# Layer 1 of a two-layer graph network: head 0's product in 4 of 32 row tiles made by the scalar engine from logits to which a DMA adds adj

## The chip, the cores and the metric

One core of one Trainium2 chip. The metric is device time in microseconds (us) of one launch; the median of three runs of the kernel before is 3041.72 us. Times inside the launch come from one profiled execution and count from the start of its span.

Engine names are those of the profile: PE is the matrix engine (PEld its weight loads), DVE the vector engine, ACT the scalar engine, POOL the GpSimd engine, SP the engine that issues most loads. Each engine takes its instructions in the order in which they stand, and waits in that order.

## The reference, cut to what matters

`x` is 4096 x 512, `adj` a 4096 x 4096 matrix of zeros and ones. Two layers follow each other. Layer 0 is an attention with one head (`L0`); the change does not touch it. Layer 1 is a graph attention with 8 heads of 64 columns:

```python
h = jnp.maximum(_layernorm(x, axis=-1), 0.0)
data1 = (h @ W.T + b).reshape(N, H, D)
src = jnp.einsum('nhd,xhd->nh', data1, src_proj)
trg = jnp.einsum('nhd,xhd->nh', data1, trg_proj)
e = src.T[:, :, None] + trg.T[:, None, :]
e = jnp.where(e >= 0, e, 0.01 * e)
e = e + connectivity[None, :, :]      # connectivity is adj here
scores = jax.nn.softmax(e, axis=-1)
out = jnp.einsum('hnm,hmd->hnd', scores, data1.transpose(1, 0, 2))
x = x + out
```

So for each head, each target row n and each source row m the kernel needs the weight exp(leaky(src_n + trg_m) + adj[n, m]), its sum over m, and its product with the 64 values of row m. The exponential splits: exp(adj) is common to the heads, and leaky's two branches become a maximum of two products of row and column factors.

## The kernel before, in words

**Tiling of layer 1.** The output is cut into 4 blocks of 1024 target rows (`WL`) and 2 sets of 4 heads (`HG`): 8 *groups*, number i. In each group a loop goes over 32 tiles of 128 source rows; the tile number is m. A *step* is one (i, m). Source rows lie on the 128 partitions, the 1024 target rows on the free axis, so every weight tile is 128 x 1024 in fp32.

**One step.** `load` (L668, SP) brings the tile of `adj_t` (512 KB) into one of three buffers `e`. `exps` (L682, ACT) makes ex = exp(adj) into PSUM; the pool `p_x` has one buffer, so ex of step m + 1 can't be written before DVE has read ex of step m for the last time. `last_exps` (L692, ACT) makes e3 = exp(adj + a column) for head 3 into SBUF. `relus` (L698, ACT) makes `rl`, a relu of head 0's row factors with a scale and a bias of one column each. `weigh` (DVE) makes the four products `pr0` to `pr3` in the order of heads 3, 0, 1, 2: L710 is (z max g) * ex, with e3 in place of ex for head 3, and L707 is (rl - ngd) * ex for head 0. Each is one instruction on 128 x 1024.

**Sums.** POOL adds up head 3's products over the steps (L719, accumulator `acc3`). Head 0's products are added up by accumulating DMAs from POOL's queue (L724, L726) into `acc00` and `acc01` in the 19 steps of `BY_DMA`: m from 2 to 26 without those with m % 4 == 1. In the other 13 steps PE takes the sum.

**gather** (PE) multiplies the four products with the values (L742, 16 matmuls that the trace records as 32 passes, banks `pv`), then takes the sums of heads 1 and 2, and of head 0 where no DMA does (L747, bank `dn`). The products of heads 3 and 0 come first, those of heads 1 and 2 after them.

**Buffers.** `pr0` and `pr3` have three buffers, `pr1` and `pr2` two; `rl`, `e3` and `acc3` two.

**Order.** It is written out by hand; nothing is planned by costs:

```python
stages = ((load, 3), (exps, 1), (weigh, 1), (factors, 2), (scale, 2), (gather, 0))
for s in range(len(steps)):
    for f, ahead in stages:
        if s + ahead < len(steps):
            f(*steps[s + ahead])
    ...
    next(ending, None)
```

`factors` is `last_exps` and then `relus`. So while DVE works at the products of step m, ACT's queue holds ex(m), e3(m+1), rl(m+1), in groups 0 and 1 two short `scale` instructions (L678), and then whatever `ending` yields. In group 0 `ending` is `tables`, which writes row factors to DRAM (`z_d`); later groups' factors are read from there by `zload` at m = 20, 22, 24, 26 (SP). In every later group it is `finish` of the group before: ACT copies `pv` (L771) and `dn` (L777) out of PSUM in the first two steps, PE makes two transposes a step, and ACT makes four short scaled copies `o` (L821) a step behind the products of steps 4 to 11; POOL issues four accumulating loads of `x1` into `o` (L824). `finish_last` ends the last group.

Of the kernel before, what the change touches and what calls it, by code (L numbers as in the profile page):

```python
# [8 lines left out]
FP = mybir.dt.float32  # L9
AF = mybir.ActivationFunctionType  # L10
ALU = mybir.AluOpType
# [4 lines left out]
P = 128  # L16
# [3 lines left out]
SLOPE = 0.01  # L20


def row_bcast(ap, n, offset=0):

    return bass.AP(tensor=ap.tensor, offset=ap.offset + offset, ap=[[0, P], [1, n]])
# [3 lines left out]
def kernel(  # L29
# [15 lines left out]
    nc = tc.nc  # L45
    N, F = x.shape
    H, D = 8, 64
    HG, WL = 4, 1024
    WT = WL // P
    NT = N // P  # L50
# [6 lines left out]
    dram = ctx.enter_context(tc.tile_pool(name="dram", bufs=1, space=DRAM))  # L57
    ident = const.tile([P, P], FP, name="ident")
# [3 lines left out]

    x1 = dram.tile([N, F], FP, name="x1")
    z_d = dram.tile([H * NT, P], FP, name="z_d")

# [11 lines left out]
    s_n = big.tile([P, H, NT], FP, name="s_n")  # L79
    t_m = big.tile([P, H, NT], FP, name="t_m")  # L80
# [15 lines left out]
    with tc.tile_pool(name="w0", bufs=1) as wp, tc.tile_pool(name="a0", bufs=2) as ap_, tc.tile_pool(  # L96
        name="a0s", bufs=8
# [144 lines left out]
    with tc.tile_pool(name="mx", bufs=1) as mxp, tc.tile_pool(name="b_a", bufs=6) as adjp, tc.tile_pool(  # L242
        name="b_e", bufs=4
    ) as esp, tc.tile_pool(name="b_m", bufs=2) as mkp, tc.tile_pool(name="b_s", bufs=2) as sp, tc.tile_pool(
        name="b_p", bufs=6, space=PSUM
# [56 lines left out]
        for n in range(-6, len(items)):  # L302
# [3 lines left out]
            if n >= 0:  # L306
                i, j, t = items[n]
# [9 lines left out]
    with tc.tile_pool(name="c_a", bufs=11) as adjp, tc.tile_pool(name="c_b", bufs=4) as ebp, tc.tile_pool(  # L317
        name="c_e", bufs=9
    ) as etp, tc.tile_pool(name="c_w", bufs=3) as wkp, tc.tile_pool(name="c_t", bufs=3) as atp, tc.tile_pool(
        name="c_m", bufs=2  # L320
    ) as mxp, tc.tile_pool(name="c_o", bufs=4) as iop, tc.tile_pool(name="c_s", bufs=2) as sp, tc.tile_pool(
        name="c_p", bufs=1, space=PSUM
    ) as p_o, tc.tile_pool(name="c_q", bufs=3, space=PSUM) as p_t, tc.tile_pool(
        name="c_r", bufs=1, space=PSUM
# [102 lines left out]
        left, scale = [], {}  # L427
# [81 lines left out]
        tmb = big.tile([P, H], FP, name="tmb")  # L509
# [38 lines left out]
        stages = ((load, 8), (turn, 3), (exps, 2), (weigh, 1), (gather, 0))  # L548
# [22 lines left out]
        pt = p_t.tile([P, BL], FP, name="pt")  # L571
# [15 lines left out]
    l1 = ctx.enter_context(tc.tile_pool(name="l1", bufs=1))  # L587
# [2 lines left out]
    d_m = l1.tile([P, H, NT], FP, name="d_m")  # L590
    ngd_m = l1.tile([P, H // HG, NT], FP, name="ngd_m")
    ld_m = l1.tile([P, H // HG, NT], FP, name="ld_m")
    d0_m = l1.tile([P, H // 2, NT, 2], FP, name="d0_m")
    d0_0 = l1.tile([P, H // 2, P // 4], FP, name="d0_0")
    zo = l1.tile([P, 3], FP, name="zo")
# [14 lines left out]

    HV = WL // BL
    JT = BL // P
    Q = P // 4
    BY_DMA = [m for m in range(2, NT - 5) if m % 4 != 1]

    with tc.tile_pool(name="p", bufs=2) as prp, tc.tile_pool(name="rl", bufs=2) as rlp, tc.tile_pool(
        name="io1", bufs=3
    ) as iop, tc.tile_pool(name="s1", bufs=1) as sp, tc.tile_pool(name="za", bufs=1) as zp0, tc.tile_pool(name="e3", bufs=2) as e3p, tc.tile_pool(  # L620
        name="zb", bufs=1
    ) as zp1, tc.tile_pool(name="e", bufs=3) as ep, tc.tile_pool(name="ac", bufs=2) as acp, tc.tile_pool(
        name="os", bufs=1
    ) as osp, tc.tile_pool(
        name="p_x", bufs=1, space=PSUM
    ) as p_x, tc.tile_pool(name="p_v", bufs=1, space=PSUM) as p_v, tc.tile_pool(
        name="p_t1", bufs=1, space=PSUM
    ) as p_t, tc.manual_schedule():
        groups = [(b, g) for b in range(N // WL) for g in range(H // HG)]
        steps = [(i, m) for i in range(len(groups)) for m in range(NT)]  # L630
        zs_, ra, ex, e3, rl, pr, acc, pv, late = {}, {}, {}, {}, {}, {}, {}, {}, {}
        ORDER = (3, 0, 1, 2)
        for t, val in ((d0_0, 0.0), (d0_m, 0.0), (zo[:, 0:2], 0.0), (zo[:, 2:3], 1.0)):
# [2 lines left out]
        def tables():  # L636

            for h in range(H):
                nc.scalar.activation(s_n[:, h, :], s_n[:, h, :], AF.Relu, bias=tmb[:, h:h + 1])
                if h % 3 == 2:  # L640
                    yield
            nc.scalar.activation(s_n, s_n, AF.Exp, scale=-(1.0 - SLOPE))
            yield
            s_f = s_n.rearrange("p h t -> p (h t)")
            for c in range(H * NT // P):
                pz = p_t.tile([P, P], FP, name="pt")
                nc.tensor.transpose(pz, s_f[:, c * P:(c + 1) * P], ident)
                yield
                zt = sp.tile([P, P], FP, name="zt", bufs=2)
                nc.scalar.copy(zt, pz)  # L650
                nc.gpsimd.dma_start(z_d[c * P:(c + 1) * P, :], zt)
            yield


        pick = sp.tile([P, 2, 4], FP, name="pick")
        row = ident.rearrange("p (r s) -> p s r", s=Q)
        nc.vector.tensor_copy(pick, row[:, 0:2, :])
        nc.vector.tensor_tensor(pick[:, 1, 0:HV], pick[:, 1, 0:HV], row[:, 2, HV:2 * HV], ALU.add)

# [5 lines left out]
        def load(i, m):  # L665
            b, g = groups[i]
            e = ep.tile([P, WL], FP, name="e")
            nc.sync.dma_start(e, adj_t[m * P:(m + 1) * P, b * WL:(b + 1) * WL])  # L668
            ra[i, m] = e
            if i + 1 < len(groups) and m in (20, 22, 24, 26):  # L670
                zload(i + 1, ORDER[(m - 20) // 2])

# [16 lines left out]
        def last_exps(i, m):  # L689
# [2 lines left out]
            nc.scalar.activation(x_, ra[i, m], AF.Exp, bias=ld_m[:, h // HG, m:m + 1])  # L692
            e3[i, m] = x_

        def relus(i, m):
            h = groups[i][1] * HG
            r = rlp.tile([P, WL], FP, name="rl")
            nc.scalar.activation(r, zs_[i, 0], AF.Relu, bias=ngd_m[:, h // HG, m:m + 1], scale=d_m[:, h, m:m + 1])  # L698
            rl[i, m] = r

        def weigh(i, m, order=ORDER):
            h = groups[i][1] * HG
            x_ = ex.pop((i, m))
            for k in order:
                w = prp.tile([P, WL], FP, name=f"pr{k}", bufs=2 if k in (1, 2) else 3)
                if k == 0:
                    nc.vector.scalar_tensor_tensor(w, rl.pop((i, m)), ngd_m[:, h // HG, m:m + 1], x_,  # L707
                                                   op0=ALU.subtract, op1=ALU.mult)
                else:
                    nc.vector.scalar_tensor_tensor(w, zs_[i, k], g_m[:, h + k, m:m + 1],  # L710
                                                   e3.pop((i, m)) if k == 3 else x_,
                                                   op0=ALU.max, op1=ALU.mult)
                pr[i, m, k] = w
            w = pr[i, m, 3]
            if m == 1:
                acc[i, 3] = acp.tile([P, WL], FP, name="acc3")
                nc.gpsimd.tensor_tensor(acc[i, 3], pr[i, 0, 3], w, ALU.add)
            elif 1 < m < NT - 1:
                nc.gpsimd.tensor_tensor(acc[i, 3], acc[i, 3], w, ALU.add)  # L719
            if m in BY_DMA:  # L720
                n = BY_DMA.index(m)
                if n < 2:
                    acc[i, 0, n] = acp.tile([P, WL], FP, name=f"acc0{n}", bufs=1)
                    nc.gpsimd.dma_start(acc[i, 0, n], pr[i, m, 0])  # L724
                else:
                    nc.gpsimd.dma_start(acc[i, 0, n % 2], pr[i, m, 0], accum_op=ALU.add)  # L726

        def gather(i, m):
            b, g = groups[i]
            last = m == NT - 1  # L730
            if m == 0:
                pv[i] = ([[p_v.tile([P, BL], FP, name=f"pv{c}{q}") for q in range(HV)] for c in range(2)],
                         p_v.tile([P, BL], FP, name="dn"))
            v, dn = pv[i]
            by_pe = [u for u in range(NT) if u not in BY_DMA]
            side = sum(u < m for u in by_pe) % 2
            for c, pair in enumerate(((3, 0), (1, 2))):
                for q in range(HV):
                    for r in (side, 1 - side):
                        k = pair[r]  # L740
                        for c0 in range(0, D, Q):
                            nc.tensor.matmul(v[c][q][r * D + c0:r * D + c0 + Q, :],  # L742
                                             va[:, m, g * HG + k, c0:c0 + Q],
                                             pr[i, m, k][:, q * BL:(q + 1) * BL], start=(m == 0), stop=last)

            def den(r, w, src, q, **fl):
                nc.tensor.matmul(dn[r * Q:r * Q + w.shape[1], :], w, src[:, q * BL:(q + 1) * BL], **fl)  # L747

            for r in (side, 1 - side):
                for q in range(HV):  # L750
                    hk = g * 2 + r
                    den(r * HV + q, d0_m[:, hk, m, :] if m else d0_0[:, hk, :], pr[i, m, r + 1], q,
                        start=(m == 0), stop=False)
            if m in by_pe:
                for q in range(HV):
                    den(side * HV + q, zo[:, 1 - side:3], pr[i, m, 0], q, start=False, stop=False)
# [126 lines left out]

        def row_factors(k):
            z = zs_[0, k]
            nc.vector.tensor_scalar(z, z, tmb[:, k:k + 1], 0.0, ALU.add, ALU.max)
            nc.scalar.activation(z, z, AF.Exp, scale=-(1.0 - SLOPE))

        row_factors(3)
        nc.vector.tensor_tensor(t_m, t_m, tmb.unsqueeze(2).to_broadcast([P, H, NT]), ALU.subtract)  # L890
        nc.vector.tensor_scalar(ld_m, t_m[:, HG - 1::HG, :], SLOPE, None, ALU.mult)
        nc.scalar.activation(g_m, t_m, AF.Exp, scale=1.0 - SLOPE)
        last_exps(0, 0)
        del ra[0, 0]
# [12 lines left out]
        factors(0, 1)  # L907
        scale(0, 1)

        stages = ((load, 3), (exps, 1), (weigh, 1), (factors, 2), (scale, 2), (gather, 0))  # L910
        for s in range(len(steps)):
            for f, ahead in stages:
                if s + ahead < len(steps):
# [44 lines left out]
```

## Time and profile before

| | us |
|---|---|
| median of three runs | 3041.72 (3041.07 to 3043.09) |
| the profiled execution's own time | 3042.05 |
| its span, first to last instruction | 3040.3 |
| first product of layer 1 | at 1791.7 |
| group 0 (m = 0 of one group to m = 0 of the next) | 154.7 |
| group 1 | 154.6 |
| groups 2 to 6, each | 153.7 |

The granted TensorE clock is 0.995 in the mean. The page gives busy times and shares of the whole span; layer 1 is its last 41%. In a row of a group, "x512 | 631.1, 1273" means 512 instructions, 631.1 us in which at least one of them ran, 1273 ns for one from start to end. Instructions of one engine overlap: the next starts before the last has ended, so the pace is read from start to start in the timeline, not from the duration.

### The profile page before, as it was taken

Reading aid. Unit: us, or ns where it says so; the run is one execution under the profiler, and the core shown is the slowest. Engines: PE = TensorE matmul, PEld = TensorE weight load, DVE = VectorE, ACT = ScalarE, POOL = GpSimd, SP = SyncE. Lnnn points to the kernel's source line nnn. Section 1 sums busy time; section 2 is a strip of 40 time slices with the busy share of each in tenths; the row PEclk is TensorE's granted clock in tenths of the full one; section 3 lists DMA queues with packets and bytes.
Section 4 is the critical chain, followed back from the end, with each engine's and each line's share of the span. In section 5 each row is a group of like instructions: output and inputs, shape, how many; then the busy total and the mean of one; then the engine's idle time right before and its main releaser. Section 6 shows DMA issues by size and latency. Waiting matters only on the chain.

```text
span 3040.3 us, 43210 instructions
## 1 busy us (share of the span) xinstructions
PE 2988.8 (98%) x15817; PEld 1204.4 (40%) x15817; DVE 2517.5 (83%) x3515; ACT 1292.0 (42%) x1819; POOL 1332.7 (44%) x1009
## 2 busy tenths in 40 slices
PE   8999999999999999999999989999999999999998
PEld 4444444444444444444444433323222222222222
DVE  5335777777677687887987789999999999999998
ACT  2111111111111121121122367887777777777775
POOL 3401111113333343443544656564656564656564
PEclk9999999999999999999999999999999999999999
DMA  4205666666444454554543238595959596968685
GB/s 152 97 4 195 223 220 224 233 211 216 139 161 161 148 175 134 173 168 142 185 167 119 63 112 213 170 230 173 233 172 232 176 227 177 228 178 224 181 216 139
DMA packets 226645, 531.51 MB, mean 175 GB/s; under 512 B 24888, under 2 KB 50520, under 8 KB 226432
## 3 DMA queue, kind: packets, MB, share of 16 engines
q1 hardware_dynamic: 178048, 384.12, 37.9%
q0 software_dynamic: 46368, 140.70, 19.6%
q10 hardware_dynamic: 2016, 3.93, 0.4%
q8 instruction: 124, 2.03, 0.3%
q14 instruction: 89, 0.73, 0.1%
HBM read 389.02 MB, written 59.93 MB: 148 GB/s over the span
## 4 chain that ended last, share of the span: by engine, by line
PE 69%; DVE 19%; ACT 6%; issue 4%; DMA 1%; DVEq 0%; SPq 0%; POOL 0%; ACTq 0%; POOLq 0%
PE po L419 29%; DVE pr L710 16%; PE pe L284 15%; PE pv L742 8%; ACT e L692 4%; PE ps L155 4%; PE po L489 4%; PE pe L162 4%; PE dn L747 3%; DVE pr L707 2%; PE pt L369 2%; ACT rl L698 1%; PE pt L797 1%; PE pt L143 0%; PE pt L481 0%
## 5 line engine op out<-in xcount | busy, mean ns | idle before, releaser
L742 PE MATMUL pv<-pr,sup 128*32 128x512 f32 x8192 | 1010.1, 595 | 17.2 <-DVE pr L710 8.4
L419 PE MATMUL po<-sup,at 128*128 128x512 f32 x2048 | 905.5, 594 | 2.8 <-DVE at L389 2.8
L719 POOL TENSOR_TENSOR acc<-acc,pr 128x1024 f32<-128x1024 f32 x232 | 555.9, 2396 | 391.3 <-DVE pr L710 390.1
L710 DVE SCALAR_TENSOR_TENSOR pr<-z,g_m,ex 128x1024 f32<-128x1024 f32 x512 | 631.1, 1273 | 3.7 <-PE dn L747 3.7
L419 PEld LDWEIGHTS po<-sup,at 128*128 128x128 f32 x2048 | 379.0, 191 | 428.6 <-issue 417.0
L399 POOL TENSOR_TENSOR racc<-racc,ex 128x512 f32<-128x512 f32 x240 | 343.0, 1429 | 452.2 <-ACT ex L383 451.0
L742 PEld LDWEIGHTS pv<-pr,sup 128*32 128x32 f32 x8192 | 287.1, 110 | 609.2 <-issue 494.9
L383 ACT ACTIVATE ex<-d 128x512 f32<-128x512 f32 x256 | 160.6, 630 | 722.8 <-DVE d L381 715.6
L682 ACT ACTIVATE ex<-e 128x1024 f32<-128x1024 f32 x256 | 263.5, 1029 | 305.4 <-DVE pr L710 305.4
L284 PE MATMUL pe<-he_t,he_t 128*128 128x512 f32 x896 | 386.4, 592 | 0.0
L707 DVE SCALAR_TENSOR_TENSOR pr<-rl,ngd_m,ex 128x1024 f32<-128x1024 f32 x256 | 326.0, 1273 | 3.3 <-ACT ex L682 3.0
L747 PE MATMUL dn<-pr,d_m 128*2 128x512 f32 x1984 | 327.3, 592 | 0.0
L710 DVE SCALAR_TENSOR_TENSOR pr<-z,g_m,e 128x1024 f32<-128x1024 f32 x256 | 326.4, 1275 | 0.2 <-ACT e L692 0.2
L698 ACT ACTIVATE rl<-z,ngd_m,d_m 128x1024 f32<-128x1024 f32 x256 | 314.3, 1228 | 0.0
L692 ACT ACTIVATE e<-e,ld_m 128x1024 f32<-128x1024 f32 x256 | 290.5, 1135 | 0.0
L381 DVE TENSOR_TENSOR d<-d,mk 128x512 f32<-128x512 f32 x256 | 269.3, 1052 | 8.8
L284 PEld LDWEIGHTS pe<-he_t,he_t 128*128 128x128 f32 x896 | 169.2, 190 | 210.1 <-issue 190.8
L287 ACT COPY es<-pe 128x512 f32<-128x512 f32 (+2 forms) x144 | 79.3, 551 | 377.0 <-PE pe L284 377.0
L288 POOL DMA_DIRECT2D e_d<-es x144 | 78.6, 546 | 364.6 <-ACT es L287 358.9
L380 DVE TENSOR_TENSOR d<-pt,mb 128x512 f32<-128x512 f32 (+2 forms) x136 | 87.4, 643 | 166.5 <-PE pt L369 166.5
L389 DVE TENSOR_TENSOR at<-ex,a 128x512 f32<-128x512 f32 x256 | 175.6, 686 | 23.1 <-ACT ex L383 21.3
L289 DVE CUSTOM_DVE_ANT_0 mk<-pe,mk 128x512 f32<-128x512 f32 (+2 forms) x144 | 93.0, 646 | 99.6 <-ACT es L287 99.6
(162 smaller groups left out, 2546.4 us busy)
## 6 DMA issues: line engine op xcount, KB each, us to landing
e<-in_adj_t_dram SPq DMA_DIRECT2D x256, 512.0 KB, 4.6
acc<-pr POOLq DMA_DIRECT2D x152, 512.0 KB, 5.2
a<-in_adj_t_dram SPq DMA_DIRECT2D x256, 256.0 KB, 3.1
ar<-in_adj_dram SPq DMA_DIRECT2D x120, 256.0 KB, 3.1
e_d<-es POOLq DMA_DIRECT2D x120, 256.0 KB, 3.2
ac<-in_adj_t_dram SPq DMA_DIRECT2D x112, 256.0 KB, 3.7
eb<-e_d SPq DMA_DIRECT2D x28, 1024.0 KB, 6.3
et<-e_d SPq DMA_DIRECT2D x112, 256.0 KB, 3.3
```

The source lines that it names most:

```text
L284: nc.tensor.matmul(pe[:, :w], he_t[i][:, k, (t % TB) * P:(t % TB + 1) * P], he_t[j][:, k, BL - w:], start=(k == 0), stop=(k == KC - 1))
L381: nc.vector.tensor_tensor(d, d, mk, ALU.add)
L399: nc.gpsimd.tensor_tensor(racc, racc, e, ALU.add)
L419: nc.tensor.matmul(po[j], w[:, j * P:(j + 1) * P], sup[:, m, :], start=(m == 0), stop=last)
L682: nc.scalar.activation(x_, ra.pop((i, m)), AF.Exp)
L692: nc.scalar.activation(x_, ra[i, m], AF.Exp, bias=ld_m[:, h // HG, m:m + 1])
L698: nc.scalar.activation(r, zs_[i, 0], AF.Relu, bias=ngd_m[:, h // HG, m:m + 1], scale=d_m[:, h, m:m + 1])
L707: nc.vector.scalar_tensor_tensor(w, rl.pop((i, m)), ngd_m[:, h // HG, m:m + 1], x_, op0=ALU.subtract, op1=ALU.mult)
L710: nc.vector.scalar_tensor_tensor(w, zs_[i, k], g_m[:, h + k, m:m + 1], e3.pop((i, m)) if k == 3 else x_, op0=ALU.max, op1=ALU.mult)
L719: nc.gpsimd.tensor_tensor(acc[i, 3], acc[i, 3], w, ALU.add)
L742: nc.tensor.matmul(v[c][q][r * D + c0:r * D + c0 + Q, :], va[:, m, g * HG + k, c0:c0 + Q], pr[i, m, k][:, q * BL:(q + 1) * BL], start=(m = ...
L747: nc.tensor.matmul(dn[r * Q:r * Q + w.shape[1], :], w, src[:, q * BL:(q + 1) * BL], **fl)
```

## The change

In steps m = 9, 13, 17, 21 of every group (`BY_LOG`) head 0's product is made in another way. `logs` makes, three steps ahead, the relu part of the logit from a row tile `u` and a column (`nlg_m`) on ACT, and an accumulating DMA from POOL's queue adds the tile of `adj_t` to it in SBUF. In `weigh`, ACT takes the exponential of that with a column as bias and writes it as `pr0`; DVE makes no product for head 0 in these steps, and `relus` is left out in them. The rest of these steps, ex and the load of `e` among it, stays.

The row tile `u` holds the relu before its exponential. For group 0 it is kept from `row_factors`; for the later groups `tables` writes it to DRAM (`u_d`: two transposes, one copy and one DMA more, and one `yield` more), and it is read back into one buffer at m = 28 of the group before, by SP.

Buffers: `pr3` goes from three to two, `acc3` from two to one, `rl` from two to three. PE's work is the same: the four steps are among those in which PE takes head 0's sum anyway.

```diff
+    u_d = dram.tile([2, NT, P], FP, name="u_d")
...
+    nlg_m = l1.tile([P, H // HG, NT], FP, name="nlg_m")
...
+    BY_LOG = (9, 13, 17, 21)
     BY_DMA = [m for m in range(2, NT - 5) if m % 4 != 1]
 
-    with tc.tile_pool(name="p", bufs=2) as prp, tc.tile_pool(name="rl", bufs=2) as rlp, tc.tile_pool(
+    with tc.tile_pool(name="p", bufs=2) as prp, tc.tile_pool(name="rl", bufs=3) as rlp, tc.tile_pool(
...
-    ) as osp, tc.tile_pool(
+    ) as osp, tc.tile_pool(name="u", bufs=1) as usp, tc.tile_pool(
...
+            pz = p_t.tile([P, 2, P], FP, name="pt")
+            for g in range(H // HG):
+                nc.tensor.transpose(pz[:NT, g, :], s_n[:, g * HG, :], ident)
+            yield
+            ut = sp.tile([NT, 2, P], FP, name="ut")
+            nc.scalar.copy(ut, pz[:NT])
+            nc.gpsimd.dma_start(u_d.rearrange("g t p -> t g p"), ut)
             nc.scalar.activation(s_n, s_n, AF.Exp, scale=-(1.0 - SLOPE))
...
+            if i + 1 < len(groups) and m == 28:
+                us[i + 1] = usp.tile([P, WL], FP, name="u")
+                b, g = groups[i + 1]
+                nc.sync.dma_start(us[i + 1], row_bcast(u_d, WL, g * N + b * WL))
...
+        def logs(i, m):
+            if m in BY_LOG:
+                b, g = groups[i]
+                r = rlp.tile([P, WL], FP, name="rl")
+                nc.scalar.activation(r, us[i], AF.Relu, bias=nlg_m[:, g, m:m + 1], scale=-(1.0 - SLOPE))
+                nc.gpsimd.dma_start(r, adj_t[m * P:(m + 1) * P, b * WL:(b + 1) * WL], accum_op=ALU.add)
+                rl[i, m] = r
+
         def relus(i, m):
+            if m in BY_LOG:
+                return
...
-                w = prp.tile([P, WL], FP, name=f"pr{k}", bufs=2 if k in (1, 2) else 3)
-                if k == 0:
+                w = prp.tile([P, WL], FP, name=f"pr{k}", bufs=3 if k == 0 else 2)
+                if k == 0 and m in BY_LOG:
+                    nc.scalar.activation(w, rl.pop((i, m)), AF.Exp, bias=t_m[:, h, m:m + 1])
+                elif k == 0:
                     nc.vector.scalar_tensor_tensor(w, rl.pop((i, m)), ngd_m[:, h // HG, m:m + 1], x_,
                                                    op0=ALU.subtract, op1=ALU.mult)
...
-                acc[i, 3] = acp.tile([P, WL], FP, name="acc3")
+                acc[i, 3] = acp.tile([P, WL], FP, name="acc3", bufs=1)
...
         def row_factors(k):
             z = zs_[0, k]
-            nc.vector.tensor_scalar(z, z, tmb[:, k:k + 1], 0.0, ALU.add, ALU.max)
-            nc.scalar.activation(z, z, AF.Exp, scale=-(1.0 - SLOPE))
+            u = z
+            if k == 0:
+                u = us[0] = usp.tile([P, WL], FP, name="u")
+            nc.vector.tensor_scalar(u, z, tmb[:, k:k + 1], 0.0, ALU.add, ALU.max)
+            nc.scalar.activation(z, u, AF.Exp, scale=-(1.0 - SLOPE))
...
+        nc.vector.tensor_scalar(nlg_m, t_m[:, 0::HG, :], -(1.0 - SLOPE), None, ALU.mult)
...
-        stages = ((load, 3), (exps, 1), (weigh, 1), (factors, 2), (scale, 2), (gather, 0))
+        stages = ((load, 3), (logs, 3), (exps, 1), (weigh, 1), (factors, 2), (scale, 2), (gather, 0))
```

In a step of `BY_LOG` ACT's queue then reads ex(m), the exponential for `pr0` (called *w* below), e3(m+1), rl(m+1); the relu of `logs` for step m (called *log*) stands ahead of ex(m-2), its DMA on POOL between the instructions for step m-3 and the addition for step m-2.

More of the change, by code (lines that the diff above doesn't have):

```diff
@@ L630 @@
         steps = [(i, m) for i in range(len(groups)) for m in range(NT)]
+        us = {}
         zs_, ra, ex, e3, rl, pr, acc, pv, late = {}, {}, {}, {}, {}, {}, {}, {}, {}
```

## The prediction

> **What bounds the kernel now.** I read the page first, then the stretches of single groups, then the timeline of one group engine by engine. The page:
>
> ```profile
> PE 2988.8 (98%) x15817; PEld 1204.4 (40%) x15817; DVE 2517.5 (83%) x3515; ACT 1292.0 (42%) x1819; POOL 1332.7 (44%) x1009
> ...
> L742 PE MATMUL pv<-pr,sup 128*32 128x512 f32 x8192 | 1010.1, 595 | 17.2 <-DVE pr L710 8.4
> L710 DVE SCALAR_TENSOR_TENSOR pr<-z,g_m,ex 128x1024 f32<-128x1024 f32 x512 | 631.1, 1273 | 3.7 <-PE dn L747 3.7
> L682 ACT ACTIVATE ex<-e 128x1024 f32<-128x1024 f32 x256 | 263.5, 1029 | 305.4 <-DVE pr L710 305.4
> L707 DVE SCALAR_TENSOR_TENSOR pr<-rl,ngd_m,ex 128x1024 f32<-128x1024 f32 x256 | 326.0, 1273 | 3.3 <-ACT ex L682 3.0
> ```
>
> DVE's products in layer 1 wait for almost nothing (3.7 and 3.3 us in all), PE nearly as little (17.2), while ACT idles 305 us, all before ex, released by DVE. So DVE is the bound with PE close behind, and ACT looks free. How free is seen in the timeline of one plain step (m = 17 of group 4), DVE and then ACT; columns are start, time, engine, line, operation:
>
> ```profile
> 2490.66 1.28 DVE L710 SCALAR_TENSOR_TENSOR pr<-z,g_m,e 128x1024 f32<-128x1024 f32 x1
> 2491.86 1.27 DVE L707 SCALAR_TENSOR_TENSOR pr<-rl,ngd_m,ex 128x1024 f32<-128x1024 f32 x1
> 2493.05 2.46 DVE L710 SCALAR_TENSOR_TENSOR pr<-z,g_m,ex 128x1024 f32<-128x1024 f32 x2
> 2495.43 1.27 DVE L710 SCALAR_TENSOR_TENSOR pr<-z,g_m,e 128x1024 f32<-128x1024 f32 x1
> ```
> ```profile
> 2490.77 1.03 ACT L682 ACTIVATE ex<-e 128x1024 f32<-128x1024 f32 x1 [1.54 <-DVE pr L710]
> 2491.73 1.13 ACT L692 ACTIVATE e<-e,ld_m 128x1024 f32<-128x1024 f32 x1
> 2492.77 1.23 ACT L698 ACTIVATE rl<-z,ngd_m,d_m 128x1024 f32<-128x1024 f32 x1
> 2495.54 1.03 ACT L682 ACTIVATE ex<-e 128x1024 f32<-128x1024 f32 x1 [1.54 <-DVE pr L710]
> ```
>
> A step lasts 4.77 us, four products of 1.19 from start to start. ACT's ex starts 0.11 after the step does, because the single buffer of ex is free only then, and the next ACT instructions follow at 0.96, 1.04 and (in the steps of `finish`, below) 1.13. DVE's head 0 product starts at 1.20, when ex ends at 1.14: ex is on the path with 0.05 us to spare, hidden by one product alone. ACT's real freedom is the 1.54 us between rl and the next ex. In the steps of `finish` it is less:
>
> ```profile
> 2458.80 1.23 ACT L698 ACTIVATE rl<-z,ngd_m,d_m 128x1024 f32<-128x1024 f32 x1
> 2459.93 0.90 ACT L821 ACTIVATE o<-pt,rd 128x64 f32<-128x64 f32 x4
> 2461.56 1.03 ACT L682 ACTIVATE ex<-e 128x1024 f32<-128x1024 f32 x1 [0.73 <-DVE pr L710]
> ```
>
> The four o take 0.80 at their pace of 0.20. PE's place: in group 4 the first pass of gather(m) starts 2.73 us after step m when PE has nothing to catch up (m = 22 to 25). The transposes of `finish` push that to 7.96 at m = 10; then it falls by 0.48 a plain step (4.29 us of PE work against 4.77) and is 3.00 at m = 21. Once in a group PE is so late that DVE waits for the buffer of pr1, at m = 12:
>
> ```profile
> 2469.18 2.47 DVE L710 SCALAR_TENSOR_TENSOR pr<-z,g_m,ex 128x1024 f32<-128x1024 f32 x2 [0.49 <-PE dn L747]
> ```
>
> From the step's length (5.35 for 4.77) that costs 0.57.
>
> **The change, part by part.** Times below count from the start of the step named.
>
> *Products removed.* 4 x 1.19 = 4.77 us of DVE a group, 38 us in eight groups. How much of it reaches the end is decided by ACT.
>
> *The exponential w in ACT's queue.* It stands between ex(m) and e3(m+1). Its nearest row is L692 (exponential, SBUF to SBUF, column bias): 1.04 from start to start; the ends are L682's 0.96 and L698's 1.13, worth 0.1 each way. The step on DVE now lasts 3 x 1.19 = 3.58, and the next ex should start at 3.69. ACT is done with its queue at 0.11 + 0.96 + 1.04 + 1.04 + 1.13 = 4.28. DVE waits 0.59 at its next head 0 product, and a plain log step saves 1.19 - 0.59 = 0.60. That holds for m = 13, 17, 21: 1.8 us a group.
>
> *m = 9 falls into `finish`.* w adds the four o: the queue ends at 5.08, a stall of 1.39, more than the 1.19 saved. The relu of log(9), 1.13 us by L698, stands before ex(7): 0.11 + 0.96 + 1.04 + 1.13 + 0.80 + 1.13 = 5.17 against 4.88, a stall of 0.28; that of log(13) before ex(11) costs 0.29 in the same way. The logs for 17 and 21 fit into the 1.54. Together 1.96 lost around m = 9.
>
> *The wait at m = 12 goes.* DVE gets there 1.96 - 1.19 = 0.77 later, PE no later than before (its 5 us of arrears at m = 9, 10 cover the delay), so the 0.57 is not waited.
>
> Sum for groups 2 to 7: 4.77 - 1.77 - 1.96 + 0.57 = 1.6 us each, 9.7 in six. PE permits about this and little more: with its 4.29 a plain step and 4.72 for one with head 0's sum, it catches up with the faster DVE at m = 26 instead of 21, and from 27 on needs 4.72 of 4.77 a step.
>
> *Groups 0 and 1* have the two `scale` instructions behind rl, 0.5 us. Group 0: each w stalls 1.09, so 4 x (1.19 - 1.09) = 0.4, less 0.1 for a log beside a table copy: 0.3 gained. Group 1 has scale and o both: stalls 0.77 (log 9), 1.89 (w at 9), 0.79 (log 13), 3 x 1.09, in all 6.7 against 4.77; its own waits for PE at m = 8 to 12, 1.06, go. It loses 0.9. The new column table at the start costs DVE some 0.15.
>
> *The accumulating load.* POOL issues it after the addition for step m-3, which ends at 3.8, and that step's own 0.86 us DMA:
>
> ```profile
> 2482.55 2.39 POOL L719 TENSOR_TENSOR acc<-acc,pr 128x1024 f32<-128x1024 f32 x1 [1.58 <-DVE pr L710]
> 2484.90 0.85 POOL L726 DMA_DIRECT2D acc<-pr  x1
> ```
>
> So at 4.7, when the relu is done too; POOL is free until 6.2, so the addition behind it isn't delayed. w wants the sum at 1.07 of step m, that is 10.7 us later. What rows exist for the landing:
>
> ```profile
> e<-in_adj_t_dram SPq DMA_DIRECT2D x256, 512.0 KB, 4.6
> acc<-pr POOLq DMA_DIRECT2D x152, 512.0 KB, 5.2
> o<-x POOLq DMA_DIRECT2D x28, 256.0 KB, 7.5
> ```
>
> Same size and accumulating: 5.2, the low end. The high end is o<-x, which accumulates from DRAM as this does, 7.5 for half the bytes, doubled to 15. I take 9.0, nearest to the acc row: 5.2, plus 2.2 for the acc transfer issued just ahead (q0: 140.70 MB in 19.6% of the span, 4.2 us a MB), plus 1.6 for an e load between (q1: 37.9% for 384 MB). That lands 1.7 us early and costs nothing. Four such loads add 8.9 us of DMA to 153.7, to a share of 0.76.
>
> *Parts at nothing.* u's load is SP's 28th-step extra; SP idles over 3 us a step and u is wanted ten steps later. `acc3` with one buffer: the first addition of a group starts at 2414.71, the last pass that reads the old sums ends at 2413.53. `pr3` with two buffers would wait where PE is latest, up to 0.7 at m = 10, and ACT's stall of 1.39 on the product after it covers that. Without ACT's stalls these 0.7 would be paid. The additional table work in group 0 lies where PE and ACT have room.
>
> A rule that speaks against the change: the Trainium skill, "SBUF — State Buffer", section "Who interferes with whom", says that a DVE instruction with two SBUF inputs and a GpSimd instruction that reads SBUF exclude each other. Head 3's product (z and e3 both in SBUF) never meets POOL's addition in this trace, since it starts at 4.77 and the addition ends at 3.8; in log steps it would start at 3.58. By the rule it waits 0.24, in 32 steps 7.7 us; but head 0's next product waits for ex until 5.37 anyway, so I get the same sum by rule and by row.
>
> **Sum.** 9.7 + 0.3 - 0.9 - 0.15 = 8.9 us. The profiled execution's 3042.05 gives 3033.1; it stands 0.33 above the median of the runs, so from the median 3032.8.
>
> **Rivals.** (1) *ACT's instructions are dearer.* w waits for several semaphores and might cost L698's whole 1.23: 0.19 more in 32 steps takes 6 us, and 3039 is left. For: no row shows such an instruction. Against: L692's pace. (2) *The accumulating load lands late*, and w blocks ACT, with e3, rl and the next ex queued behind it and DVE behind these. One us late is 32 us: 3065; at the doubled o<-x landing (15, 4.3 late) 3170. It decides from 8.9 / 32 = 0.28 us of mean lateness, a landing at 11.0. For: DMA share 0.78 in a group's first half, o<-x's 7.5. Against: the acc row, and that o<-x moves 1 KB pieces where this moves 4 KB ones. (3) *The whole DVE saving arrives*, 38 us, 3003.6. Against: ACT's queue, and PE, whose spare time after m = 21 is about 2 us a group.
>
> **How the numbers follow.** Some 0.2% (6 us) is what a measurement of this kernel can tell from no change. The forecast has 0.57, (1) 0.19, (2) 0.20, (3) 0.04. Faster by over 0.2%: the forecast and (3), 0.61; within 0.2%: (1) 0.19; slower: (2) 0.20. The range runs from 3028 (ACT at its cheap end, PE's limit of about 2 us a group) past (1), 3039, to 3046, which is (2) with 0.4 us of mean lateness; what is left out is the rest of (2) and (3).
>
> **What would show it right or wrong.** Right: log steps of 3.58 and next ones of 5.36; the idle time before L682 falls by some 40 us, DVE's waits for ex rise by about 33 (6 x 3.7, 4.5 and 6.7); groups 2 to 6 last 152.1, group 1 155.5; m = 10 lasts over 6 us if PE doesn't hold m = 9. Wrong: a wait of ACT's w for the DMA (rival 2), groups above 153.7; or DVE's waits for PE in place of those for ex, with groups near 152; or log steps followed by 4.77 (rival 3).

## The result, and the profile after

The changed kernel takes 3039.65 us (median of 12 runs, 3036.68 to 3044.28); the kernel before, timed beside it, 3041.55 (12 runs, 3041.07 to 3043.32). The ratio is 0.9992 with an interval of [0.9983, 1.0001]: a gain of 1.9 us, within what can't be told from no change, where 8.9 were forecast. The profiled execution took 3040.68 us, its span is 3038.8.

The page after, the groups that answer to those of before (L739 is the product pr = (z max g) * ex, L736 head 0's product, L699 ex, L709 e3):

```profile
PE 2988.1 (98%) x15819; PEld 1206.2 (40%) x15819; DVE 2487.0 (82%) x3484; ACT 1317.7 (43%) x1852; POOL 1362.1 (45%) x1042
...
L739 DVE SCALAR_TENSOR_TENSOR pr<-z,g_m,ex 128x1024 f32<-128x1024 f32 x512 | 631.3, 1274 | 6.8 <-PE dn L776 6.8
L699 ACT ACTIVATE ex<-e 128x1024 f32<-128x1024 f32 x256 | 262.8, 1027 | 260.2 <-DVE pr L739 260.0
L736 DVE SCALAR_TENSOR_TENSOR pr<-rl,ngd_m,ex 128x1024 f32<-128x1024 f32 x224 | 285.8, 1276 | 29.0 <-ACT ex L699 26.8
L709 ACT ACTIVATE e<-e,ld_m 128x1024 f32<-128x1024 f32 x256 | 291.3, 1138 | 16.8 <-DMA e<-in_adj_t_dram 16.5
```

Read the last two columns. DVE has 32 products fewer and is busy 30.5 us less, and in exchange its head 0 product waits 26.8 us for ex (3.0 before). ACT's idle time before ex fell by 45 us. Both were forecast. The last line was not: ACT waits 16.5 us for the tiles of `e`, the ordinary loads of adj. Before, its idle time there was nothing:

```profile
L692 ACT ACTIVATE e<-e,ld_m 128x1024 f32<-128x1024 f32 x256 | 290.5, 1135 | 0.0
```

Step by step, the length of a step being the time from one head 3 product to the next. One log step and the step after it (group 4, m = 17 and 18), DVE and then ACT:

```profile
2492.96 1.28 DVE L739 SCALAR_TENSOR_TENSOR pr<-z,g_m,e 128x1024 f32<-128x1024 f32 x1
2494.16 2.47 DVE L739 SCALAR_TENSOR_TENSOR pr<-z,g_m,ex 128x1024 f32<-128x1024 f32 x2
2496.54 1.62 DVE L739 SCALAR_TENSOR_TENSOR pr<-z,g_m,e 128x1024 f32<-128x1024 f32 x1
2498.29 1.28 DVE L736 SCALAR_TENSOR_TENSOR pr<-rl,ngd_m,ex 128x1024 f32<-128x1024 f32 x1
```
```profile
2493.08 1.03 ACT L699 ACTIVATE ex<-e 128x1024 f32<-128x1024 f32 x1 [2.67 <-DVE pr L739]
2494.04 1.14 ACT L734 ACTIVATE pr<-rl,t_m 128x1024 f32<-128x1024 f32 x1
2495.08 1.14 ACT L709 ACTIVATE e<-e,ld_m 128x1024 f32<-128x1024 f32 x1
2496.12 1.23 ACT L725 ACTIVATE rl<-z,ngd_m,d_m 128x1024 f32<-128x1024 f32 x1
2497.25 1.01 ACT L699 ACTIVATE ex<-e 128x1024 f32<-128x1024 f32 x1
```

The log step lasts 3.58 us (2492.96 to 2496.54), the next one 5.34, to 2501.88. *w* (L734) starts 1.08 after its step and holds ACT for 1.04. All of this is as forecast. Now group 6, m = 14, where it is not:

```profile
2784.10 1.00 ACT L699 ACTIVATE ex<-e 128x1024 f32<-128x1024 f32 x1
2786.37 1.15 ACT L709 ACTIVATE e<-e,ld_m 128x1024 f32<-128x1024 f32 x1 [1.26 <-DMA e<-in_adj_t_dram]
2787.42 1.23 ACT L725 ACTIVATE rl<-z,ngd_m,d_m 128x1024 f32<-128x1024 f32 x1
2788.56 1.14 ACT L716 ACTIVATE rl<-u,nlg_m 128x1024 f32<-128x1024 f32 x1
2789.59 1.01 ACT L699 ACTIVATE ex<-e 128x1024 f32<-128x1024 f32 x1
```

e3 waits 1.26 us for its tile, and everything behind it in ACT's queue, the log's relu among it, comes later: ex(15) starts at 2789.59 where DVE had read the old ex for the last time at 2788.79. So DVE idles:

```profile
2790.63 1.28 DVE L736 SCALAR_TENSOR_TENSOR pr<-rl,ngd_m,ex 128x1024 f32<-128x1024 f32 x1 [0.64 <-ACT ex L699]
```

Against the kernel before, step by step, the unforeseen lengthening lies at m = 15 (0.35 to 1.04 in groups 1 to 7, 5.2 us together), at m = 11 (up to 1.24, part of it made good at m = 13, where PE holds DVE less), and at m = 23 (0.3 in two groups).

Where the transfers stand is read from the windows view, group 6, the stretch from m = 10 to 20 (columns: stretch, length, busy time of each engine, granted clock, DMA busy share, GB/s), before and then after:

```profile
2762.00:2810.00 48.00, 48.00 (x444) 13.96 (x440) 47.51 (x41) 34.52 (x43) 31.85 (x20) 1.00 0.91 231
```
```profile
2762.00:2810.00 48.00, 48.00 (x440) 13.83 (x436) 45.29 (x38) 38.11 (x46) 34.65 (x23) 1.00 1.06 271
```

The prediction used 0.76, the share of a whole group. In this third it was 0.91 before the change and is 1.06 now; in the 46 us ahead of it the share is 0.67, in the 59 us behind it 0.77. That last mean hides a second full stretch: in m = 20 to 24, where rows of z are loaded, the windows view gives 0.92 before and 1.04 after (group 6). The DMA view of the same 48 us of the kernel after (tile, issuer, count, size, median us from issue to landing):

```profile
e<-in_adj_t_dram SPq DMA_DIRECT2D x10, 512.0 KB, 7.2
acc<-pr POOLq DMA_DIRECT2D x7, 512.0 KB, 7.4
rl<-in_adj_t_dram POOLq DMA_DIRECT2D x3, 512.0 KB, 8.6
```

The same view of the kernel before has, for the first two:

```profile
e<-in_adj_t_dram SPq DMA_DIRECT2D x10, 512.0 KB, 5.2
acc<-pr POOLq DMA_DIRECT2D x7, 512.0 KB, 5.2
```

The accumulating load itself lands after 8.6 (9.0 in the median of all 32), as forecast. It is the e tiles beside it that are late: the slowest of the ten takes 10.1 us, against 7.7 before. What a load of e may take follows from the order: its buffer is free after ex(m) and e3(m+3) reads it two steps later. From issue to reader that is 9.45 us in plain steps. If one of the two is a log step it is 8.8 to 9.05, measured in x9_half below, where no e3 waits; the short step and the longer one behind it take that much away.

### The profile page after: what moved, and what is told of

It reads as the page before. It is cut to its first block, busy times and chain, and to the rows that moved or that the text cites. A ratio compares the mean times of both kernels' runs of the same rounds, so it can differ in the third digit from the quotient of the medians.

```text
span 3038.8 us, 43237 instructions
## 1 busy us (share of the span) xinstructions
PE 2988.1 (98%) x15819; PEld 1206.2 (40%) x15819; DVE 2487.0 (82%) x3484; ACT 1317.7 (43%) x1852; POOL 1362.1 (45%) x1042
## 4 chain that ended last, share of the span: by engine, by line
PE 65%; DVE 15%; ACT 8%; DMA 7%; issue 4%; POOL 0%; DVEq 0%; SPq 0%; ACTq 0%; POOLq 0%
PE po L420 29%; PE pe L285 15%; DVE pr L739 12%; DMA e<-in_adj_t_dram 6%; PE pv L771 5%; PE po L490 4%; PE ps L156 4%; PE pe L163 4%; ACT e L709 3%; DVE pr L736 2%; PE dn L776 2%; PE pt L370 2%; ACT ex L699 2%; ACT rl L725 2%; DMA rl<-in_adj_t_dram 1%
## 5 line engine op out<-in xcount | busy, mean ns | idle before, releaser
L748 POOL TENSOR_TENSOR acc<-acc,pr 128x1024 f32<-128x1024 f32 x232 | 564.6, 2433 | 320.4 <-DVE pr L739 316.7
L739 DVE SCALAR_TENSOR_TENSOR pr<-z,g_m,ex 128x1024 f32<-128x1024 f32 x512 | 631.3, 1274 | 6.8 <-PE dn L776 6.8
L699 ACT ACTIVATE ex<-e 128x1024 f32<-128x1024 f32 x256 | 262.8, 1027 | 260.2 <-DVE pr L739 260.0
L739 DVE SCALAR_TENSOR_TENSOR pr<-z,g_m,e 128x1024 f32<-128x1024 f32 x256 | 328.5, 1283 | 0.3 <-ACT e L709 0.2
L736 DVE SCALAR_TENSOR_TENSOR pr<-rl,ngd_m,ex 128x1024 f32<-128x1024 f32 x224 | 285.8, 1276 | 29.0 <-ACT ex L699 26.8
L709 ACT ACTIVATE e<-e,ld_m 128x1024 f32<-128x1024 f32 x256 | 291.3, 1138 | 16.8 <-DMA e<-in_adj_t_dram 16.5
L725 ACT ACTIVATE rl<-z,ngd_m,d_m 128x1024 f32<-128x1024 f32 x224 | 275.2, 1229 | 0.0
```

The costliest lines, as they stand in the source:

```text
L699: nc.scalar.activation(x_, ra.pop((i, m)), AF.Exp)
```

## The experiments

The theory after reading the traces: the four accumulating loads overfill the DMA engines in m = 10 to 20, e tiles land late, and ACT, which around log steps has no slack, passes that on. Rivals: the fewer buffers cost it; *w* costs by its place in ACT's queue; the load costs by its number or its place in POOL's queue, not its bytes; e is late only because DVE now runs ahead of its loads. Every ratio is against the kernel before on the same chip. "Groups" are groups 2 to 6, 153.7 us before.

| run | median us | ratio, interval | groups, us | ACT's waits for e, us |
|---|---|---|---|---|
| after | 3039.65 | 0.9992 [0.9983, 1.0001] | 152.8 to 154.1 | 16.5 |
| x1_thin | 3032.52 | 0.9969 [0.9957, 0.9981] | 152.0 | none |
| x9_half | 3032.37 | 0.9968 [0.9956, 0.9981] | 152.0 | none |
| x10_extra | 3043.69 | 1.0007 [0.9998, 1.0015] | 153.7 to 154.0 | 17.2 |
| x4_bufs | 3041.46 | 0.9999 [0.9990, 1.0008] | 153.7 | none |
| x2_e4 | 3039.52 | 0.9994 [0.9985, 1.0003] | 152.1 to 154.0 | none |
| x3_early | 3041.91 | 0.9999 [0.9991, 1.0008] | 152.6 to 155.2 | 18.8 |
| x5_two | 3034.62 | 0.9977 [0.9968, 0.9986] | 152.4 to 152.9 | 5.7 |
| x6_late4 | 3034.64 | 0.9977 [0.9969, 0.9986] | 151.2 to 153.0 | 9.8 |
| x7_early_thin | 3020.59 | 0.9929 [0.9916, 0.9941] | 151.1 to 151.4 | none |
| x8_two_early | 3028.18 | 0.9955 [0.9942, 0.9967] | 151.9 | none |
| x11_two_25 | 3024.77 | 0.9942 [0.9928, 0.9955] | 151.4 | 1.3 |

### x1_thin: the load moves 16 columns

```diff
-                nc.gpsimd.dma_start(r, adj_t[m * P:(m + 1) * P, b * WL:(b + 1) * WL], accum_op=ALU.add)
+                nc.gpsimd.dma_start(r[:, 0:16], adj_t[m * P:(m + 1) * P, b * WL:b * WL + 16], accum_op=ALU.add)
```

> The accumulating DMA of the four log steps moves 16 columns of the adj_t tile where it moved 1024 (adj is added in these 16 alone); every instruction, wait and buffer stays. Theory A (the four extra 512 KB transfers a group delay the loads of the next adj_t tiles, and ACT's e3 waits for them at m = 11, 15 and 23): ACT's waits for e, 16.5 us in the changed kernel, go; groups 2 to 6 last 152.1 and group 1 155.5, as the prediction's sum had them; about 3033 us. Theory B (what is lost at m = 11 and 15 is POOL's: its queue waits for the relu of a log step and issues the transfers behind it late, whatever their size): m = 11 and 15 stay long, groups at 153, 3039 us.

Instructions, waits and queue places stay; only bytes go. It takes 3032.52 us, every one of groups 2 to 6 lasts 152.03, and L709 has no idle time left:

```profile
L709 ACT ACTIVATE e<-e,ld_m 128x1024 f32<-128x1024 f32 x256 | 291.1, 1137 | 0.0
```

The prediction's number was 3032.8 and 152.1. So its sum for ACT, DVE and PE holds to 0.3 us, and the 7 us missing in the changed kernel are the bytes of 32 transfers.

### x9_half: the load moves 512 of 1024 columns

```diff
-                nc.gpsimd.dma_start(r, adj_t[m * P:(m + 1) * P, b * WL:(b + 1) * WL], accum_op=ALU.add)
+                nc.gpsimd.dma_start(r[:, 0:512], adj_t[m * P:(m + 1) * P, b * WL:b * WL + 512], accum_op=ALU.add)
```

> The changed kernel whose accumulating load moves 512 of the 1024 columns, so adj reaches half of head 0's columns in the four steps; everything else stays. A dose between the whole load (3039.7, DMA busy share 1.04 in m = 10 to 20) and 16 columns (3032.5, 0.96). If the DMA engines are full in m = 10 to 20 and the lateness of e comes from there: share near 1.00, waits of e3 for e fewer and shorter than the 16.5 us of the changed kernel, 3033 to 3037. If the accumulating load costs by its number or by its place in POOL's queue, not by its bytes: within 1 us of 3039.7.

3032.37 us: all of the gain with half of the bytes, a little below the range expected. The price is not in proportion to the bytes; it sets in between half and whole. The same stretch of group 6 (m = 10 to 20), thin and then half:

```profile
2755.00:2803.00 48.00, 48.00 (x440) 13.83 (x436) 46.29 (x39) 39.30 (x47) 35.78 (x23) 1.00 0.95 237
```
```profile
2755.00:2803.00 48.00, 48.00 (x442) 13.93 (x444) 46.29 (x39) 39.32 (x48) 35.77 (x23) 1.00 1.01 254
```

At 254 GB/s the median e load there takes 6.8 us and the slowest 8.2, inside the 8.8 to 9.05 that it has; at 271 GB/s the slowest takes 10.1. It is close: over groups 2 to 6 of x9_half the tightest load (the tile of m = 23, group 5) takes 8.7 of its 8.84 us. A load may get later for nothing until it reaches the time at which it is read.

### x10_extra: the transfers alone

```diff
-    BY_LOG = (9, 13, 17, 21)
+    BY_LOG = ()
+    EXTRA = (9, 13, 17, 21)
...
+        scrap = usp.tile([P, WL], FP, name="scrap")
+        nc.gpsimd.memset(scrap, 0.0)
+        def extra(i, m):
+            if m in EXTRA:
+                b, g = groups[i]
+                nc.gpsimd.dma_start(scrap, adj_t[m * P:(m + 1) * P, b * WL:(b + 1) * WL], accum_op=ALU.add)
...
-        stages = ((load, 3), (logs, 3), (exps, 1), (weigh, 1), (factors, 2), (scale, 2), (gather, 0))
+        stages = ((load, 3), (extra, 3), (exps, 1), (weigh, 1), (factors, 2), (scale, 2), (gather, 0))
```

> The kernel before in its products (head 0 always on DVE, w and the relu of logs left out), but POOL issues the four accumulating loads of 512 KB a group into a tile that nobody reads, at the same steps and the same three steps ahead. So the transfers alone, at the old pace of DVE. If the transfers themselves delay e: waits of ACT for e near m = 11, 15, 23, groups of 153.9 to 154.8, 3043 to 3049. If e is late only because DVE runs ahead of the loads in the changed kernel: no such waits, groups of 153.7, 3041 to 3042.

Of the two expectations neither came whole. The transfers alone make e as late in total as in the changed kernel; this is its waits view from 1950 us on (groups 1 to 7; group 0 adds one wait of 2.3):

```profile
ACT e L710 <- DMA e<-in_adj_t_dram: 14.8, 15, 1.9
```

So DVE's faster pace isn't needed to make e late. It does shift the place: at m = 14, right behind a log step, ACT waits 8.1 us in the changed kernel and 3.1 here; at m = 22 it is 5.6 and 9.5. But groups 3, 4 and 6 last 153.7 as before, and all eight together are only 1.9 us longer than before, 1.2 of them at m = 23 of group 0. One of these waits, in group 4:

```profile
2477.63 1.15 ACT L710 ACTIVATE e<-e,ld_m 128x1024 f32<-128x1024 f32 x1 [0.32 <-DMA e<-in_adj_t_dram]
2478.69 1.23 ACT L734 ACTIVATE rl<-z,ngd_m,d_m 128x1024 f32<-128x1024 f32 x1
2481.05 1.03 ACT L700 ACTIVATE ex<-e 128x1024 f32<-128x1024 f32 x1 [1.14 <-DVE pr L748]
```

The 0.32 us are taken out of the idle time ahead of ex, 1.14 instead of 1.54, and ex starts on time. In the kernel with the old pace 17.2 us of lateness cost about 2; in the changed one 16.5 cost 7.8 (its eight groups against those of x9_half), because w and the relu of log fill that idle time around a log step. The same place shows it: at m = 14 a wait of 1.86 us makes the next step 0.39 longer here (group 7), and waits of 0.90 to 1.57 make it 0.35 to 1.04 longer in the changed kernel, where the relu of log(17) stands ahead of ex(15).

### x2_e4: a fourth buffer for e

```diff
-    with tc.tile_pool(name="p", bufs=2) as prp, tc.tile_pool(name="rl", bufs=3) as rlp, tc.tile_pool(
+    with tc.tile_pool(name="p", bufs=2) as prp, tc.tile_pool(name="rl", bufs=2) as rlp, tc.tile_pool(
...
-    ) as zp1, tc.tile_pool(name="e", bufs=3) as ep, tc.tile_pool(name="ac", bufs=2) as acp, tc.tile_pool(
+    ) as zp1, tc.tile_pool(name="e", bufs=4) as ep, tc.tile_pool(name="ac", bufs=2) as acp, tc.tile_pool(
...
+        load(0, 3)
...
-        stages = ((load, 3), (logs, 3), (exps, 1), (weigh, 1), (factors, 2), (scale, 2), (gather, 0))
+        stages = ((load, 4), (logs, 3), (exps, 1), (weigh, 1), (factors, 2), (scale, 2), (gather, 0))
```

> Four buffers for the tiles e and their loads one step earlier (rl goes from three buffers to two to make room); the transfers' bytes are those of the changed kernel. Theory A: a tile is asked for 4.8 us earlier and was at most 1.9 us late, so ACT's waits for e go and the time is about 3033 us, groups 2 to 6 at 152.1. Theory C (the DMA engines are full from m = 10 to 17 and a deeper queue only moves the lateness, to the sums of head 0's products or to the log step's own transfer): part of the stalls stay, 3036 to 3040 us, with DVE or ACT waiting for other transfers.

The loads of e start a step earlier and no e3 waits, yet the time stays at 3039.52 us. Groups range from 152.1 to 154.0, because now *w* waits for its own load, and DVE's head 0 product for a buffer of pr0 that a late sum (acc<-pr) still reads. Both are theory C. From the waits view (groups 1 to 7):

```profile
ACT rl L725 <- DVE pr L736: 10.5, 28, 1.1
ACT pr L734 <- DMA rl<-in_adj_t_dram: 5.4, 6, 1.4
DVE pr L736 <- DMA acc<-pr: 1.9, 3, 0.7
```

The DMA share in the stretch is 1.05. Room for one stream moves the wait to another, as long as the stretch stays as full. The first line is the price of two buffers for `rl` and not of the DMA: mostly 0.3 us a time, with which steps keep their length (group 0 and m = 7, 11 and 19 of the others). What part it has in the longer steps was not separated.

### x4_bufs: no log steps, the buffers and u alone

```diff
-    BY_LOG = (9, 13, 17, 21)
+    BY_LOG = ()
```

> Buffers alone: no log step at all, but two buffers for pr3, one for acc3, three for rl, and u made and loaded. The prediction's term: with two buffers pr3 waits for PE where PE is latest, up to 0.7 us at m = 10 to 12, of which the wait for pr1 behind it takes over all but 0.2: 3042 to 3044 us with the u loads. Rival: the buffers cost nothing, 3041.6 us.

3041.46 us, groups 153.70 to 153.71. In each group m = 11 is 0.47 longer and m = 12 as much shorter: DVE's wait for PE at the buffer of pr1 becomes one at that of pr3 a step earlier. Two buffers for head 3's products cost nothing, with no stall of ACT there to cover them.

### x3_early: w ahead of ex

```diff
+        def logprod(i, m):
+            if m in BY_LOG:
+                h = groups[i][1] * HG
+                w = prp.tile([P, WL], FP, name="pr0", bufs=3)
+                nc.scalar.activation(w, rl.pop((i, m)), AF.Exp, bias=t_m[:, h, m:m + 1])
+                pr[i, m, 0] = w
...
-        stages = ((load, 3), (logs, 3), (exps, 1), (weigh, 1), (factors, 2), (scale, 2), (gather, 0))
+        stages = ((load, 3), (logs, 3), (logprod, 1), (exps, 1), (weigh, 1), (factors, 2), (scale, 2), (gather, 0))
```

> The exponential w of a log step stands ahead of ex of the same step in ACT's queue, where the left-out rl leaves room, and not behind it. ACT theory (the 0.57 us after each log step and the 1.0 to 1.4 at m = 10 are ACT's queue): the step after a log step lasts 4.77 where PE is not late; the gain is capped by PE at about 2 us a group against before, and the late e tiles stay: 3034 to 3037 us. PE theory (PE's arrears set the end of a group and ACT's stalls cost nothing): the waits only change their name, from ex to PE's sums, 3039 us. A risk: w now wants the sum 3.7 us earlier, and may wait for the DMA and hold ex.

*w* fills ACT's idle time in the step before instead of standing between ex and e3. By itself it gains nothing, 3041.91 us: it wants its load some 3.7 us earlier (2.65 ahead of its step in x11_two_25 below, where nothing holds it, instead of 1.08 after) and waits for it, which was the risk named (groups 1 to 7; in the whole layer 53.8 us, and another 9 for PE to free a buffer of pr0).

```profile
ACT pr L732 <- DMA rl<-in_adj_t_dram: 47.1, 20, 4.1
```

### x7_early_thin: w ahead of ex, 16 columns

The edits of x1_thin and x3_early together.

> w ahead of ex, and the accumulating DMA moves 16 columns alone (adj is added in these alone): the ACT stalls after log steps and the transfer's bytes are both taken away, so what is left is PE's cap. PE's spare time in the kernel before, from its 4.29 and 4.72 us a step against 4.77, is about 2.2 us a group: groups 2 to 6 at 151.5, group 0 (no transposes) 4.5 shorter, 3020 to 3024 us. If w ahead of ex still holds DVE up (for the buffer of pr0, or for the small transfer's landing): groups at 152 or more, 3028 to 3033 us.

3020.59 us. Against x1_thin that is 11.9 us less: the price of *w*'s place between ex and e3, as far as PE lets it show. ACT now gives nothing back of the 1.19 us that a log step saves, 4.77 a group, but groups 2 to 6 still last 151.1 to 151.4, only 2.3 to 2.6 less than before: most of the rest comes back as waits of DVE for PE, 12.3 us in the eight groups (3.7 before), all at m = 9 to 13. This is PE's limit, which the prediction put at about 2 us a group: from 2716 to 2869 us, longer than a group, PE is busy for all 153.00 us (151.57 before).

```profile
sum 153.00, PE 153.00 PEld 48.48 DVE 150.75 ACT 116.53 POOL 96.03; mean PE 51.00 PEld 16.16 DVE 50.25 ACT 38.84 POOL 32.01
```

### x5_two and x6_late4: other steps

```diff
-    BY_LOG = (9, 13, 17, 21)
+    BY_LOG = (17, 21)
```

for x5_two, and for x6_late4

```diff
-    BY_LOG = (9, 13, 17, 21)
+    BY_LOG = (17, 21, 25, 29)
...
-            if i + 1 < len(groups) and m == 28:
+            if i + 1 < len(groups) and m == 31:
```

> Log steps at m = 17 and 21 alone. Capacity theory (between m = 10 and 20 the DMA engines are already nine tenths busy before the change, and the two loads for m = 13 and 17 with that for 9 drive them over what they can move): with one of those three left the e tiles come in time, each log step saves 0.6 us as in the run with the thin transfer, nothing is lost around m = 9: groups 2 to 6 at 152.5, groups 0 and 1 0.3 shorter together, 3034 us. If it is not the amount in that stretch but any such transfer ahead of an e load: e waits stay near m = 15 to 19 and 23, groups 153 or more, 3037 to 3040 us.

> Four log steps again, with the same bytes, at m = 17, 21, 25 and 29 (u is read back at m = 31 and not at 28, since it is used longer). Capacity theory: the last third of a group has room on the DMA engines, so the same four transfers cost much less there; PE caps the gain near 1.7 to 2 us a group: groups 2 to 6 at 151.8 to 152.3, 3030 to 3034 us. If four such transfers cost the same wherever they stand: 3039 us.

With half of the log steps the kernel is faster than with all: 3034.62 us. The steps at m = 9 and 13 gave little (x1_thin, which has them and no bytes, is 152.0 a group, x5_two 152.4 where e3's waits cost nothing), and their transfers fall into the long full stretch. There, in m = 10 to 20, the share is now 0.96 and no e3 waits. The 5.7 us of waits that are left all stand at m = 22 of groups 2 to 6, in the second full stretch (share 1.04 in m = 20 to 24 of group 6, where x9_half, without waits, has 0.99), and lengthen two steps, by 0.45 and 0.28. Moving all four later gives the same 3034.64, just past the range hoped for: e3 waits for the tiles of m = 23 and 27 (0.3 to 2.1 us, six steps 0.5 to 1.6 longer), where `zload` reads four rows of z in m = 20 to 26. In m = 20 to 28 the share is 1.02, in m = 10 to 20 it is 0.97 (group 6): the full stretch has moved along with the loads.

### x8_two_early and x11_two_25: two log steps, w ahead of ex, logs four ahead

```diff
-    BY_LOG = (9, 13, 17, 21)
+    BY_LOG = (17, 21)
...
-        stages = ((load, 3), (logs, 3), (exps, 1), (weigh, 1), (factors, 2), (scale, 2), (gather, 0))
+        stages = ((load, 3), (logs, 4), (logprod, 1), (exps, 1), (weigh, 1), (factors, 2), (scale, 2), (gather, 0))
```

with `logprod` as in x3_early; this is x8_two_early, and x11_two_25 has (17, 25) in place of (17, 21).

> Log steps at m = 17 and 21, w ahead of ex, the log relu and its DMA one step earlier (four steps ahead), so that w gets its sum in time. Two products of 1.19 come off DVE a group and no ACT stall follows: 2.2 to 2.4 us a group up to PE's cap, groups 2 to 6 at 151.5, groups 0 and 1 2.4 shorter: 3024 us. If the transfers are late here too: ACT's w waits for the DMA, ex and DVE behind it, 3030 us or more.

3028.18 us, not the 3024 expected; groups 2 to 6 all last 151.93. Of two savings of 1.19 us one is given back by half: m = 18 is 0.56 longer, since the relu of log(21), four steps ahead, stands in the short step 17.

> As x8_two_early (two log steps a group, w ahead of ex, the logs four steps ahead) with m = 17 and 25 in place of 17 and 21, so that no log's relu stands in a log step. If the 0.56 us at m = 18 of x8_two_early came from that relu: it goes, groups 2 to 6 at 151.2 to 151.5 (the cap of PE by x7_early_thin is 151.1), 3023 to 3025. If e is late behind the second load in m = 22 to 26, where z is loaded too: waits of e3 for e there, 151.7 to 152.5, 3026 to 3030.

3024.77 us, groups 151.43 to 151.45. At m = 17 and at m = 25 the step loses 1.19, and no step gets longer for it. ACT around m = 17 of group 4, with *w* (L732) in the step before:

```profile
2480.03 1.13 ACT L732 ACTIVATE pr<-rl,t_m 128x1024 f32<-128x1024 f32 x1
2482.80 1.03 ACT L699 ACTIVATE ex<-e 128x1024 f32<-128x1024 f32 x1 [1.63 <-DVE pr L746]
...
2486.38 1.03 ACT L699 ACTIVATE ex<-e 128x1024 f32<-128x1024 f32 x1 [0.35 <-DVE pr L746]
```

ACT waits for DVE before both ex, 1.63 and 0.35 us: at neither is it the later one. This version beats both kernels, 16.6 us under the kernel before by the medians, with half of the change's log steps.

## Why the prediction was right and wrong, step by step

**The step that failed is "The accumulating load", by its clauses "costs nothing" and "to a share of 0.76".** The transfer's own landing was forecast at 9.0 us after its issue and was 9.0 in the median; *w* started 1.07 to 1.10 after its step in 31 of 32 cases and at 1.27 in one. The 9.0 is luck in part, for the row that it was built on, acc<-pr, itself went from 5.2 to 7.2. But the step asked only whether this load is in time for *w*, and priced its effect on the others by a mean over the group. The mean was wrong too: 0.76 is the share of a group before the change, and 8.9 of 153.7 us more make it 0.82. In m = 10 to 20 the share was already 0.91, and it went to 1.06; the loads of e there went from 5.2 to 7.2 us in the median, the slowest to 10.1, past the 8.8 to 9.5 that they have. Measured price: 7.1 us by the medians of after and x1_thin, 7.8 by the groups of after and x9_half. It was put at 0.

**The rest of the sum was right, with some errors that cancel.** Without the bytes it is 3032.5 (x1_thin) for 3032.8. Groups 2 to 6: 152.03 for 152.1. In a plain log step 3.58 and then 5.34 for 3.58 and 5.36. At m = 9 the parts fell otherwise than told: the step lasts 4.34, not 3.58, because PE holds DVE for 0.68 us there, and ACT's stall in the next is 0.6 and not 1.39; the two together come to +0.18 for +0.20. The stall at m = 7, 0.18 for 0.28, and the one at m = 11, 0.20 for 0.29, were a little smaller, and the wait at m = 12 went with its 0.57. But PE holds DVE a step later instead: in x1_thin the log step m = 13 lasts 4.36, and it and the next save 0.41 together and not 0.60. DVE's waits for ex rose by 24 us for the 33 forecast, but only by 15 in x1_thin: PE's holds at m = 9 and 13 took the place of the rest, and the other 8.5 of the 24 come from the late e.

**Groups 0 and 1** were off by 0.3 to 0.4 us each way: 0.6 gained for 0.3 in group 0, and in group 1 0.5 lost for 0.9 without the bytes (1.6 with them). The column table `nlg_m` was put at 0.15; the start of layer 1 lies 0.7 later, but already the work of layer 0 before it ends that much later, and x4_bufs and x10_extra, which make the same table, start at 1792.4 and 1790.2: it is below what one execution shows.

**"Without ACT's stalls these 0.7 would be paid"** is wrong: x4_bufs has no such stall and pays nothing.

**The rule on the shared port.** The Trainium skill, "SBUF — State Buffer", section "Who interferes with whom", was weighed as a wait of 0.24. The case occurs as described: the head 3 product after a log step starts (2496.54) while POOL's addition still runs.

```profile
2494.68 2.40 POOL L748 TENSOR_TENSOR acc<-acc,pr 128x1024 f32<-128x1024 f32 x1 [1.86 <-DVE pr L739]
```

The addition ends at 2497.08. In the records the product starts on time, but it takes 1.62 us instead of 1.28, and ends 1.08 after the addition. Most overlaps are shorter, some 0.25 us, and make it 1.33, which again ends 1.08 after the addition. So it is throughout: in all 151 cases of these runs with an overlap of 0.23 or more the product ends 1.08 to 1.09 us after the addition, and in the 26 with 0.16 or less it takes its 1.28. That agrees with the page's rule of an exclusive lock, if the first 0.2 us of the product's record need no shared port; this last is a reading of the numbers and no run separates it. The delay, 0.05 us in most cases and not 0.24, is covered: head 0's next product starts at 2498.29, right after ex.

**The rivals.** (1) named the time, 3039, by coincidence, and was wrong in its reason: *w* costs L692's pace, 1.04, and none of L698's 1.23. (2) had the right resource and the right queue, a late load that blocks ACT and DVE behind it, but the wrong load: e3 waited for e, *w* for nothing. x3_early and x2_e4 show *w* waiting as (2) says, once it stands earlier or the e loads do. (3) did not come in any version: x7_early_thin, with ACT's price gone, ends at 3020.6, and DVE waits for PE there.

What stays open: why the landing rises as steeply as it does between 254 and 271 GB/s was not taken apart, and neither was whether a plain load in place of the accumulating one would fill the engines less.

## What to carry to other kernels

Judge a new transfer by the DMA share of the stretch that it falls into and not of the loop, and ask of every other load there how long it may take, by its buffers and the order of its reader, before asking whether the new one is in time. A late load costs only what its reader's engine has no idle time for, so a change that moves work to an engine and adds transfers at once spends the same slack twice: price both against one account. Where a replacement gives back half of what it saves in some steps, do fewer of them, in the steps where nothing is given back, and put the new instruction into the idle time ahead of the critical one.

## What the runs showed of the hardware that was not expected

The accumulating load's time to landing grows slowly with its size: 5.9 us for 8 KB (x1_thin), 7.3 for 256 KB (x9_half), 9.0 for 512 KB (after), all medians. In these three an accumulating transfer of 512 KB was issued from POOL's queue at most 3.4 us earlier. In x11_two_25 the last one was issued 5.7 us earlier or more, and the same 512 KB land in 6.0 us in the median (5.6 to 8.4). So much of the 9.0 may belong to the transfer ahead; no run changed that alone.

The lateness has a threshold in these runs: DMA shares of 0.95 and 1.01 in m = 10 to 20 (x1_thin, x9_half) cost the same, nothing, and 1.06 came with the 7 us in layer 1. A share above 1 means that the recorded times of packets overlap; 271 GB/s were still moved.
